# A graph layer on one core: 44 node columns a step instead of 40, three register loads on VectorE instead of two, and a gather ring of twenty

## The chip, the cores and the metric

The kernel runs on one core of a Trainium2 chip. The metric is device time in microseconds (us), from one launch to its end; the median of three runs of the kernel before is 1898.23 us (1897.33 to 1900.16). The profile was taken from one further execution. The engines are TensorE (PE, its weight loads PEld), VectorE (DVE), ScalarE (ACT), GpSimd (POOL) and SyncE (SP). Each engine has a sequencer, which reads the instruction stream in order, executes register loads, register arithmetic and semaphore instructions itself, and passes the rest to its engine; the profile marks the sequencer's own entries with a q (DVEq).

## The reference

One message-passing layer over 12500 nodes of 64 features and 212500 edges that are sorted by destination (`dst`), a residual and a layer norm:

```python
msg_in = concatenate([nodes[row], nodes[col], edge_features])        # 64 + 64 + 32 per edge
messages = relu(msg_in @ mW1 + mb1) @ mW2 + mb2                      # 160 -> 128 -> 64
aggregated = segment_sum(messages, col, num_segments=12500)
upd_in = concatenate([nodes, aggregated])
y = relu(upd_in @ uW1 + ub1) @ uW2 + ub2
out = layernorm(x + y)                                               # row = src, col = dst
```

Everything is float32. `mW2` is applied after the sum over edges, so the kernel sums the 128 hidden values of each edge and counts the edges of each node.

## The kernel before

**Tiling.** The 212500 edges are cut into G = 554 groups of 384 edges (TG = 3 tiles of 128). Because the edges are sorted by destination, the destinations of a group lie in a window of W = 32 nodes. Four groups (SB = 4) make a block, whose transposed edge features are loaded by one DMA into a buffer `own.st` (a ring of BLOCKS = 3).

**Two ways for source features to arrive.** The 64 features of each edge's source node come by an indirect DMA from GpSimd, one for each tile of 128 edges (`gather`, L149), into the ring `own.s`, from where TensorE turns (transposes) them (L341) and ScalarE copies them into `own.st` (L351). For some groups, listed in `COPIED`, the first tile is not gathered. Its 128 columns of 64 features are copied one at a time, 64 partitions by 4 bytes, from the node table `own.xc`, which holds all node features transposed in SBUF, straight to their place in `own.st` (`fetch`: VectorE at L503, ScalarE at L505). Where a column is to be read from is known only at run time, so a register load (L490) first brings a number of addresses from SBUF into the engine's registers, one register for one column. A step k from BEGIN = 18 on copies COLS = 40 columns: VectorE 8 and 12 (`VCOLS`, two register loads), ScalarE 12 and 8 (`ACOLS`). A copied group so comes every 128/40 = 3.2 steps, until step 544 (G - SHORT); `COPIED` has 164 groups, and 3 x 553 + 2 - 164 = 1497 gathers are left. The addresses of SPAN = 8 steps come together by a small DMA on SyncE's queue (`indexes`) and are made into byte addresses by one VectorE instruction (`addresses`, L473).

**A step.** In the main loop step k gives TensorE one run of instructions: the turn of group k, the hidden layer of group k - 2 (L366, then Relu on ScalarE, L377) and the sums of group k - 4 (L394, and the counts of edges L399). Only the last instruction of a run is waited for. On VectorE a step is, in program order:

- in one step of four, `places`: a register load of four window positions (L301) and four copies of window columns (L308);
- a piece of the update of a finished chunk of 512 nodes, if one is due (`update`, L413 to L458; 25 chunks in all);
- `add` of group k - 4: the sums are added into `agg` (L406), the counts into a row of `own.xc` (L407), both at a position held in a register;
- in one step of four, the copies of four window matrices (L320);
- the one-hot of group k + 2 (L329), which TensorE needs in step k + 2;
- `fetch(k)`: a load of 8 registers and 8 copies, a load of 12 registers and 12 copies. ScalarE's 12 and 8 are emitted right behind.

**Rings and waits.** `gather(k + AHEAD)` is emitted at the end of step k, with AHEAD = 4 and RING = AHEAD + 4 = 8 buffers; it waits for the turn of an earlier group that used the buffer, taken at the second of a pair of groups (L157). Waits between engines are partly set by hand (`after`) and otherwise found by the framework, which also orders the two engines' writes into the same `own.st` buffer. The last SHORT = 10 steps copy no columns and run the sums and hidden parts closer together.

Of the kernel before, what the change touches and what calls it, by code (L numbers as in the profile page):

```python
# [14 lines left out]
AF = mybir.ActivationFunctionType  # L15
ALU = mybir.AluOpType
# [7 lines left out]
D = 64  # L24
# [7 lines left out]
GE = TG * P  # L32
G = (E + GE - 1) // GE
SB = 4
AHEAD = 4
RING = AHEAD + 4
BLOCKS = 3
NW = 2 * SB
# [8 lines left out]
TIMES = 4  # L47
BEGIN = 18
CHECKED = 8
VCOLS = (8, 12)  # L50
ACOLS = (12, 8)
COLS = sum(VCOLS + ACOLS)
SPAN = 8
# [55 lines left out]
def ordered(ctx: ExitStack, tc: tile.TileContext, a, own, ok):  # L109
# [25 lines left out]
    def after(first, *others):  # L135

        tc.declare_no_dep(first.ins, group="quiet", reason="waits for the last of a step")
        for i in others:
            tc.add_manual_dep(
                first.ins, i.ins.name,  # L140
                mybir.DependencyInfo(mybir.DependencyClass.Sync, mybir.DependencyReason.DATA),
                reason="the kernel's own rings",
            )
        return first

    def gather(g):
        s = own.s[g % RING]
        loads[g] = [
            nc.gpsimd.indirect_dma_start(  # L149
                out=s[:p, j, :D], out_offset=None, in_=x[:, :],  # L150
                in_offset=bass.IndirectOffsetOnAxis(
                    ap=src_sb[:p, g * TG + j : g * TG + j + 1], axis=0),
            )
            for j, p in enumerate(tiles_of(g)) if j or g not in columned
        ]
        for i in loads[g]:
            after(i, *([turn_by[g // 2 * 2 + 1 - RING]] if g >= RING else []))  # L157


    iota_i = const.tile([P, W], F32, name="iota_i")  # L160
# [174 lines left out]
    def turn(g, ps):  # L335


        s = own.s[g % RING]
        xt = ps[0][: D + W, :GE]
        did = [  # L340
            nc.tensor.transpose(xt[:, j * P : j * P + p], s[:p, j, :], ident[:p, :p])  # L341
            for j, p in enumerate(tiles_of(g))
        ]

        def copy(step):
            t, c, n = columns(g)
            turn_by[g] = step
            whole = [(slice(D + W), slice(n))]
            apart = [(slice(D, D + W), slice(P)), (slice(D + W), slice(P, n))]
            copies = [  # L350
                after(nc.scalar.activation(t[r, c : c + n][:, m], xt[r, m], AF.Copy), step)  # L351
                for r, m in (apart if g in columned else whole)
            ]
            if g >= BLOCKS * SB:
                after(copies[0], hidden_by[g - BLOCKS * SB])
            copy_by[g] = copies
            return copies

        return did, [*loads.pop(g), places_by[g]], copy
# [27 lines left out]
    def sums(g, ps):  # L387
        h, s = own.h[g % NH], own.s[g % RING]
        sizes = tiles_of(g)
        sg = ps[2][:, : TIMES * W].rearrange("p (t w) -> p t w", w=W)  # L390
        counted = ps[2][0:1, TIMES * W :][:, :W]
        did = []
        for j, p in enumerate(sizes):
            did.append(nc.tensor.matmul(  # L394
                sg, h[:p, j, :],
                s[:p, j, D:].unsqueeze(1).to_broadcast([p, TIMES, W]),
                start=j == 0, stop=j == len(sizes) - 1))
        for j, p in enumerate(sizes):
            did.append(nc.tensor.matmul(counted, own.one[:p], s[:p, j, D:],  # L399
                                        start=j == 0, stop=j == len(sizes) - 1))  # L400

        def add(step):
            sums_by[g] = step
            at = bass.ds(starts.pop(g), W)
            return [
                after(nc.vector.tensor_tensor(agg[:, at], sg[:, 0, :], agg[:, at], ALU.add), step),  # L406
                after(nc.vector.tensor_tensor(xc[D : D + 1, at], counted,  # L407
                                              xc[D : D + 1, at], ALU.add), step),
            ]

        return did, [*relu_by[g], *copy_by[g]], add

# [49 lines left out]
    def indexes(i):  # L462

        n = min(SPAN * COLS, P * len(COPIED) - i * SPAN * COLS)
        if n > 0:
            indices[i] = ixp.tile([1, SPAN * COLS], I32, name="index")
            nc.sync.dma_start(indices[i][:, :n], a["src_copied"][:, i * SPAN * COLS :][:, :n])

    def addresses(i):

        if i in indices:
            t = indices[i][:, : min(SPAN * COLS, P * len(COPIED) - i * SPAN * COLS)]
            nc.vector.tensor_scalar(t, t, 4.0, float(own.at), ALU.mult, ALU.add)  # L473

    def fetch(k):

        i, n = divmod(k - BEGIN, SPAN)
        if i < 0:
            return
        if n == 0:  # L480
            indexes(i + 1)
        if n == SPAN - 2:
            addresses(i + 1)
        c0 = (k - BEGIN) * COLS
        for engine, count in [*((ET.DVE, c) for c in VCOLS), *((ET.Activation, c) for c in ACOLS)]:
            count = min(count, P * len(COPIED) - c0)
            if count <= 0:
                return
            b = c0 - i * SPAN * COLS
            _, v = nc.values_load_multi_w_load_instructions(  # L490
                indices[i][0:1, b : b + count], engines=[engine],
                min_val=own.at, max_val=own.at + 4 * (N - 1),
                skip_runtime_bounds_check_because="a source is one of the nodes",
            )
            for q, at in zip(range(c0, c0 + count), v):
                g, c = COPIED[q // P], q % P
                t, first_c, _ = columns(g)
                o = t.bitcast(U8)[:D, 4 * (first_c + c) : 4 * (first_c + c + 1)]
                x_at = xc_bytes[:D, bass.ds(at - own.at, 4)]
                by = columns_by.setdefault(g, {})  # L500
                new = engine not in by
                if engine == ET.DVE:
                    by[engine] = nc.vector.tensor_copy(o, x_at)  # L503
                else:
                    by[engine] = nc.scalar.activation(o, x_at, AF.Copy)  # L505
                after(by[engine], *([hidden_by[g - BLOCKS * SB]] if new else []))
            c0 += count

    waiting = [(closes, update(base, p, n)) for base, p, n, closes in PLAN]
    now = []  # L510
# [13 lines left out]
    def step(*work):  # L524


        parts, used = [], []
        for part, g in work:
            ps, old = own.ps[g % 2], users[part][g % 2]
            parts.append((part, g, *part(g, ps)))  # L530
            used += old
        did = [i for p in parts for i in p[2]]
        after(did[0], *used, *(i for p in parts for i in p[3]))
        copies = None
        for part, g, *_ in parts:
            if part is sums:
                for b in [b for b in xws if (b - 1) * SB <= g][:1]:
                    last, copies = windows(b, own.ps[g % 2][2][:, (TIMES + 1) * W :][:, :H])
                    did.append(last)
        for i in did[:-1]:  # L540
            tc.no_tile_sem_insts.add(i.ins.name)
            tc.add_to_no_dep_group("quiet", i.ins)
        for part, g, _, _, follow in parts:
            if part is sums:
                step_update(g)
            users[part][g % 2] = follow(did[-1])
            if part is sums and copies:
                copies()
                users[part][g % 2] += [wm_by[b * SB + i] for i in range(min(SB, G - b * SB))]
# [6 lines left out]
    windows(0, ups.tile([H, CH], F32, name="u_ps")[:, :H], False)[1]()  # L556
    indexes(0)
    made = summed = 0

    for k in range(G):  # L560
        if k < BITS:
            bit(k)
        if k == CHECKED:
            addresses(0)
            combined()
            ordered_edges()
            early.close()
            up = ctx.enter_context(tc.tile_pool(name="upd", bufs=2))
        if k % SB == 2:
            inputs(k // SB + 2)  # L570
        if k % SB == 1:
            places(k // SB + 1)
        if k < G - SHORT:
            step((turn, k), *([(hidden, k - 2)] if k > 1 else []),
                 *([(sums, k - 4)] if k > 3 else []))
            made, summed = max(0, k - 1), max(0, k - 3)
        else:

            step((turn, k))
            for _ in range(2):  # L580
                if summed < made:
                    step((sums, summed))
                    summed += 1
            for _ in range(2):
                if made <= k:
                    step((hidden, made))
                    made += 1
        onehot(k + 2)
        fetch(k)
        if k + AHEAD < G:  # L590
            gather(k + AHEAD)
    while summed < G:
# [332 lines left out]
```

## Time and profile before

| what | us |
|---|---|
| median of three runs | 1898.23 |
| the profiled execution, its own time | 1895.48 |
| its span, first to last instruction | 1893.5 |
| VectorE busy | 1492.9 (79%) |
| ScalarE busy | 1550.7 (82%) |
| GpSimd busy | 1417.6 (75%) |
| TensorE busy | 1361.4 (72%) |

The granted TensorE clock is 0.969 on average. The rows of the profile name an instruction by its line, its engine, what it writes and reads, and its count; "idle before" is the time in which the engine stood still ahead of these instructions, with what ended it ("issue": nothing that the profile shows). The sequencer's instructions do not count as busy.

### The profile page before, as it was taken

To read this page: it belongs to the slowest core of one execution; us is meant where nothing else is said; L and a number is where in the kernel's file an instruction comes from. 1 tells how busy PE (TensorE), PEld (TensorE's weight loads), DVE (VectorE), ACT (ScalarE), POOL (GpSimd) and SP (SyncE) were. 2 spreads that over 40 slices of the span, in tenths; PEclk is the share of its full clock that TensorE was granted. 3 is DMA by queue.
4 is the path that set the end of the run, shared out by engine and by line. 5 is a ranking of instruction groups with operands and counts; after the bars stand their busy time and mean duration, and the time that the engine had idled before them with its cause. 6 is when DMAs were issued, how large, how long until landed. Compare 5 with 4: busy or idle time off the path is not lost. (4 is left out here: it accounts for less than half of the span.)

```text
span 1893.5 us, 58044 instructions
## 1 busy us (share of the span) xinstructions
PE 1361.4 (72%) x12209; PEld 1193.4 (63%) x12209; DVE 1492.9 (79%) x13761; ACT 1550.7 (82%) x11818; POOL 1417.6 (75%) x1504
## 2 busy tenths in 40 slices
PE   3776777677777777677676776877767767767777
PEld 3666666666666666666665666666666656666665
DVE  3578888778888788887888878878888887888873
ACT  3489889888888888988988888889888888898882
POOL 7777777777777777777777777777777777777774
PEclk9999999999999999999999999999999999999999
DMA  6322222222222222222222222222222222222221
GB/s 136 73 46 45 46 48 44 50 43 48 46 45 48 47 43 50 45 46 44 48 50 43 48 46 45 46 48 44 50 44 47 47 48 44 47 44 50 44 47 29
DMA packets 68440, 92.50 MB, mean 49 GB/s; under 512 B 30893, under 2 KB 38350, under 8 KB 68078
## 3 DMA queue, kind: packets, MB, share of 16 engines
q0 software_dynamic: 47904, 49.12, 14.7%
q1 hardware_dynamic: 19260, 39.12, 7.4%
q14 instruction: 260, 2.13, 0.4%
q8 instruction: 102, 1.67, 0.4%
q10 hardware_dynamic: 914, 0.46, 0.1%
HBM read 85.29 MB, written 3.20 MB: 47 GB/s over the span
## 5 line engine op out<-in xcount | busy, mean ns | idle before, releaser
L149 POOL DMA_INDIRECT own_s<-in_x,src_sb x1497 | 1416.8, 946 | 457.3 <-issue 407.5
L503 DVE COPY own_st<-own_xc 64x4 uint8 x10500 | 897.7, 190 | 231.0 <-issue 217.9
L505 ACT ACTIVATE own_st<-own_xc 64x4 uint8 x10492 | 1057.1, 194 | 18.2 <-issue 15.2
L341 PE MATMUL own_ps<-own_ident,own_s 128*96 128x128 f32 x1661 | 289.5, 285 | 496.0 <-DMA own_s<-in_x,src_sb 157.9
L341 PEld LDWEIGHTS own_ps<-own_ident,own_s 128*96 128x96 f32 x1661 | 169.3, 132 | 566.1 <-ACT own_h L377 240.7
L394 PE MATMUL own_ps<-own_s,own_h 128*128 128x128 f32 x3322 | 480.5, 283 | 4.1 <-ACT own_h L377 2.9
L366 PE MATMUL own_ps<-own_wm,own_st 128*128 128x128 f32 x3322 | 479.4, 283 | 0.0
L351 ACT ACTIVATE own_st<-own_ps 96x384 f32<-96x384 f32 (+2 forms) x718 | 293.2, 408 | 205.8 <-PE own_ps L399 104.7
L394 PEld LDWEIGHTS own_ps<-own_s,own_h 128*128 128x128 f32 x3322 | 432.6, 199 | 6.3 <-ACT own_h L377 4.7
L366 PEld LDWEIGHTS own_ps<-own_wm,own_st 128*128 128x128 f32 x3322 | 432.1, 199 | 1.4 <-issue 0.5
L377 ACT ACTIVATE own_h<-own_ps 128x384 f32<-128x384 f32 x553 | 263.9, 477 | 16.0 <-PE own_ps L366 16.0
L399 PE MATMUL own_ps<-own_s,own_one 128*1 128x32 f32 x3322 | 190.1, 194 | 0.0
L320 DVE COPY own_wm<-own_ps 32x128 f32<-32x128 f32 x550 | 156.9, 285 | 5.6
L399 PEld LDWEIGHTS own_ps<-own_s,own_one 128*1 128x1 f32 x3322 | 114.5, 84 | 69.4 <-issue 6.2
L329 DVE TENSOR_TENSOR own_s<-iota,dlc 128x96 f32<-128x96 f32 x554 | 142.4, 258 | 14.3 <-issue 0.2
L406 DVE TENSOR_TENSOR agg<-own_ps,agg 128x32 f32 x554 | 105.1, 190 | 59.5 <-PE own_ps L399 25.9
L407 DVE TENSOR_TENSOR own_xc<-own_ps,own_xc 1x32 f32 x554 | 101.2, 183 | 30.6 <-PE u_ps L425 11.4
L308 DVE COPY xw<-own_xc 66x32 f32 x554 | 73.0, 207 | 15.5 <-DMA own_xc<-in_xT 9.8
L315 PE MATMUL own_ps<-w1b,xw 66*128 66x128 f32 (+1 forms) x276 | 69.1, 333 | 0.0
L446 ACT ACTIVATE rstd<-mv,eps 128x4 f32<-128x4 f32 (+1 forms) x25 | 7.4, 297 | 55.3 <-DVE mv L444 55.3
L437 PE MATMUL u_ps<-u,u 128*128 128x64 f32 (+1 forms) x196 | 50.1, 399 | 0.5 <-ACT u L427 0.5
L437 PEld LDWEIGHTS u_ps<-u,u 128*128 128x128 f32 (+1 forms) x196 | 47.1, 324 | 2.2 <-ACT u L427 0.9
(62 smaller groups left out, 276.7 us busy)
## 6 DMA issues: line engine op xcount, KB each, us to landing
own_st<-in_efT SPq DMA_DIRECT2D x138, 192.0 KB
own_s<-in_x,src_sb POOLq DMA_INDIRECT x1497
xin<-in_x SPq DMA_DIRECT2D x24, 128.0 KB
out<-o SPq DMA_DIRECT2D x24, 128.0 KB
own_xc<-in_xT SPq DMA_DIRECT2D x12, 179.2 KB
index<-in_src_copied SPq DMA_DIRECT2D x65, 1.2 KB
dlc_i<-in_dst_cols SPq DMA_DIRECT2D x1, 831.0 KB
own_xc<-in_xT SPq DMA_DIRECT2D x4, 179.5 KB
```

The source lines that it names most:

```text
L149: nc.gpsimd.indirect_dma_start(out=s[:p, j, :D], out_offset=None, in_=x[:, :], in_offset=bass.IndirectOffsetOnAxis(ap=src_sb[:p, g * TG + ...
L320: c = nc.vector.tensor_copy(wm[g % NW][D : D + W, :], wp[i * W : (i + 1) * W, :])
L329: places_by[g] = nc.vector.tensor_tensor(own.s[g % RING][:, :, D:], iota.unsqueeze(1).to_broadcast([P, TG, W]), dlc[:, g * TG : (g + 1) * ...
L341: nc.tensor.transpose(xt[:, j * P : j * P + p], s[:p, j, :], ident[:p, :p])
L351: after(nc.scalar.activation(t[r, c : c + n][:, m], xt[r, m], AF.Copy), step)
L366: nc.tensor.matmul(pre[:p, j, :], t[:, c + j * P : c + j * P + p], wm[g % NW], start=True, stop=True)
L377: relu_by[g] = [nc.scalar.activation(h, pre, AF.Relu)]
L394: did.append(nc.tensor.matmul(sg, h[:p, j, :], s[:p, j, D:].unsqueeze(1).to_broadcast([p, TIMES, W]), start=j == 0, stop=j == len(sizes) - 1))
L399: did.append(nc.tensor.matmul(counted, own.one[:p], s[:p, j, D:], start=j == 0, stop=j == len(sizes) - 1))
L406: after(nc.vector.tensor_tensor(agg[:, at], sg[:, 0, :], agg[:, at], ALU.add), step),
L503: by[engine] = nc.vector.tensor_copy(o, x_at)
L505: by[engine] = nc.scalar.activation(o, x_at, AF.Copy)
```

## The change

`COLS` goes from 40 to 44: VectorE copies 8, 8 and 8 columns a step in place of 8 and 12, ScalarE 12 and 8 as before. The three VectorE parts no longer stand together at the end of the step: the first is emitted between the two additions of `add`, the second after the step's window copies and ahead of the one-hot, the third after the one-hot. `indexes` and `addresses` of the next eight steps move behind the step's columns. AHEAD becomes 16 and the ring 20 buffers, and a gather waits for the turn of exactly the group that last used its buffer. The copies into `own.st` (L351, L503, L505) are put into a group within which the framework makes no dependencies, apart from the one on the same engine's preceding copy; the waits set by hand for TensorE's read of the buffer stay.

```diff
-AHEAD = 4
+AHEAD = 16
 RING = AHEAD + 4
-VCOLS = (8, 12)
+VCOLS = (8, 8, 8)
 ACOLS = (12, 8)
...
+    before = {}
+
+    def ordered_by_steps(i):
+
+        engine = i.ins.engine
+        tc.declare_no_dep(i.ins, group="features", keep=before.get(engine, []),
+                          reason="TensorE's step has read what the last turn of the ring wrote")
+        tc.add_to_no_dep_group("features", i.ins)
+        before[engine] = [i.ins]
+        return i
...
-            after(i, *([turn_by[g // 2 * 2 + 1 - RING]] if g >= RING else []))
+            after(i, *([turn_by[g - RING]] if g >= RING else []))
...
-                after(nc.scalar.activation(t[r, c : c + n][:, m], xt[r, m], AF.Copy), step)
+                ordered_by_steps(
+                    after(nc.scalar.activation(t[r, c : c + n][:, m], xt[r, m], AF.Copy), step))
...
-            return [
-                after(nc.vector.tensor_tensor(agg[:, at], sg[:, 0, :], agg[:, at], ALU.add), step),
-                after(nc.vector.tensor_tensor(xc[D : D + 1, at], counted,
-                                              xc[D : D + 1, at], ALU.add), step),
-            ]
+            a = after(nc.vector.tensor_tensor(agg[:, at], sg[:, 0, :], agg[:, at], ALU.add), step)
+            if between:
+                between.pop()()
+            return [a, after(nc.vector.tensor_tensor(xc[D : D + 1, at], counted,
+                                                     xc[D : D + 1, at], ALU.add), step)]
...
-    def fetch(k):
+    def fetch(k, *parts):
...
-        if n == 0:
-            indexes(i + 1)
-        if n == SPAN - 2:
-            addresses(i + 1)
-        c0 = (k - BEGIN) * COLS
-        for engine, count in [*((ET.DVE, c) for c in VCOLS), *((ET.Activation, c) for c in ACOLS)]:
+        all_parts = [*((ET.DVE, c) for c in VCOLS), *((ET.Activation, c) for c in ACOLS)]
+        for part in parts:
+            engine, count = all_parts[part]
+            c0 = (k - BEGIN) * COLS + sum(c for _, c in all_parts[:part])
...
-                after(by[engine], *([hidden_by[g - BLOCKS * SB]] if new else []))
-            c0 += count
+                ordered_by_steps(after(by[engine],
+                                       *([hidden_by[g - BLOCKS * SB]] if new else [])))
...
         if k < G - SHORT:
+            between.append(lambda: fetch(k, 0))
             step((turn, k), *([(hidden, k - 2)] if k > 1 else []),
                  *([(sums, k - 4)] if k > 3 else []))
             made, summed = max(0, k - 1), max(0, k - 3)
+            if between:
+                between.pop()()
+            fetch(k, 1)
...
         onehot(k + 2)
-        fetch(k)
+        if k < G - SHORT:
+            fetch(k, *range(2, len(VCOLS + ACOLS)))
+            if k >= BEGIN and (k - BEGIN) % SPAN == 0:
+                indexes((k - BEGIN) // SPAN + 1)
+            if k >= BEGIN and (k - BEGIN) % SPAN == SPAN - 2:
+                addresses((k - BEGIN) // SPAN + 1)
         if k + AHEAD < G:
             gather(k + AHEAD)
```

More of the change, by code (lines that the diff above doesn't have):

```diff
@@ L558, in ordered @@
     made = summed = 0
+    between = []
     for k in range(G):
```

## The prediction

> **What bounds the kernel now.** I read the page first, then the gathers by their line, the stretches of the run, and VectorE's groups within the stretch that copies columns.
>
> ```profile
> PE 1361.4 (72%) x12209; PEld 1193.4 (63%) x12209; DVE 1492.9 (79%) x13761; ACT 1550.7 (82%) x11818; POOL 1417.6 (75%) x1504
> DVE  3578888778888788887888878878888887888873
> POOL 7777777777777777777777777777777777777774
> ...
> L505 ACT ACTIVATE own_st<-own_xc 64x4 uint8 x10492 | 1057.1, 194 | 18.2 <-issue 15.2
> ```
>
> No engine is over 82% busy, but GpSimd's digits are level throughout, which is how an engine looks that never stops.
>
> ```profile
> L149 POOL DMA_INDIRECT own_s<-in_x,src_sb x1497: 901/944/1612, 2.9 to 1874.8; - x188
> ...
> POOL own_s L149 <- issue: 407.5, 1337, 0.3
> ```
>
> The 1497 gathers start between 2.9 and 1874.8 us: 1871.9/1496 = 1.2513 us from one to the next, and the pause between two is never over 0.3 us. GpSimd is full. At 40 columns a step it asks for (3 - 40/128) x 1.2513 = 3.363 us a step.
>
> ```profile
> core 0: us, PE busy (x) PEld busy (x) DVE busy (x) ACT busy (x) POOL busy (x), PEclk, DMA share, GB/s
> 80.50:1846.50 1766.00, 1284.51 (x11580) 1128.05 (x11580) 1443.02 (x13533) 1513.13 (x11756) 1335.65 (x1413) 0.97 0.22 46
> 0.00:80.50 80.50, 43.06 (x357) 38.35 (x358) 33.90 (x151) 26.77 (x37) 59.77 (x68) 0.96 0.53 116
> 1846.50:1893.50 47.00, 33.84 (x273) 27.05 (x272) 15.96 (x79) 10.78 (x26) 22.22 (x24) 0.92 0.14 29
> ```
>
> The stretch that copies columns lasts 1766.0 us. VectorE made 10500 copies, 20 a step, so it holds 525 steps of 3.364 us, which is the gathers' rate. Now VectorE's groups within that stretch:
>
> ```profile
> L503 DVE COPY own_st<-own_xc 64x4 uint8 x10500 | 897.7, 190 | 231.0 <-issue 217.9 <-ACT own_h L377 3.0 <-ACT own_st L351 0.5
> L320 DVE COPY own_wm<-own_ps 32x128 f32<-32x128 f32 x524 | 149.5, 285 | 5.3
> L329 DVE TENSOR_TENSOR own_s<-iota,dlc 128x96 f32<-128x96 f32 x525 | 135.3, 258 | 13.7 <-issue 0.2
> L406 DVE TENSOR_TENSOR agg<-own_ps,agg 128x32 f32 x525 | 99.5, 190 | 18.5 <-PE u_ps L424 9.7 <-PE own_ps L315 6.2 <-PE own_ps L399 1.8
> L407 DVE TENSOR_TENSOR own_xc<-own_ps,own_xc 1x32 f32 x525 | 95.9, 183 | 29.1 <-PE u_ps L425 10.7 <-DVE agg L406 1.0 <-issue 0.7
> L439 DVE TENSOR_TENSOR y<-u_ps,xin 128x256 f32<-128x256 f32 x23 | 9.8, 424 | 18.3 <-PE u_ps L437 18.2
> ```
>
> If the gathers alone set the pace, VectorE would stand at L406, its first wait for TensorE's step. It stands there 18.5 us in 525 steps. Its idle time is 1766.0 - 1443.0 = 323 us, of which 217.9 lie ahead of the columns and wait for nothing. So VectorE is nearly full too: at most (1766.0 - 18.5)/525 = 3.33 us a step are its own. **The two engines are in balance**, and relief for GpSimd that is paid by VectorE must be costed on VectorE.
>
> **What VectorE does in the unnamed time.** The chain of waits between 1831 and 1847 us runs on VectorE alone:
>
> ```profile
> 1832.39 0.21 DVE own_st L503 x3
> 1832.61 0.49 issue
> 1833.10 0.51 DVE own_st L503 x6
> ...
> 1839.89 0.07 DVEq L301
> ...
> 1840.80 0.20 DVE agg L406
> ```
>
> Beside it stand the register loads L490 that began in three narrow windows of this stretch, the load of four registers, and the eight copies in the order of time:
>
> ```profile
> L490 DVEq TENSOR_LOAD <-index x1: 598/598/598, 1831.3 to 1831.3; - x1
> L490 DVEq TENSOR_LOAD <-index x1: 844/844/844, 1832.2 to 1832.2; - x1
> L490 DVEq TENSOR_LOAD <-index x1: 595/595/595, 1833.9 to 1833.9; - x1
> ...
> L301 DVEq TENSOR_LOAD <-start_i x139: 340/344/594, 13.8 to 1863.6; - x139
> ...
> 1831.94 0.67 DVE L503 COPY own_st<-own_xc 64x4 uint8 x8
> ```
>
> A load of 8 takes 0.595 us, of 12 0.844, of 4 0.344: some 0.062 us a register and 0.095 for the load. Between the first two loads (1831.3 + 0.598 to 1832.2, starts to a tenth) the sequencer passed on 8 copies in 0.3 us, 0.04 each. VectorE executes one in about 0.07 (eight in 0.67, the last being 0.15 long). Then the 12-load keeps the sequencer to 1833.04, the queued copies run out at 1832.61, and VectorE idles 0.49 us until 1833.10. **The load is serial time of the sequencer**, hidden only as far as queued work lasts.
>
> **The sequencer's sum for a step.** From 1833.04 to the next load at 1833.9 are 0.87 us for 12 copies (0.48), both additions with their register arithmetic and the one-hot: 0.39 for the latter. `places` takes from 1839.89 to 1840.80, 0.91 us in one step of four, 0.23 a step; four window copies at 0.04 in one step of four, 0.04. Before: 0.595 + 0.844 + 20 x 0.04 + 0.39 + 0.23 + 0.04 = 2.90 us. After: 3 x 0.595 + 24 x 0.04 + 0.39 + 0.23 + 0.04 = **3.41 us**. Splitting the 12-load and adding four registers costs 3 x 0.595 - 1.439 = 0.35; four copies more, 0.16.
>
> The gathers would then need (3 - 44/128) x 1.2513 = 3.324 us a step. The bare sequencer sum is already over that, and over today's 3.364.
>
> **What comes on top.** Before, VectorE's own 3.33 less 2.90 leaves 0.43 us a step that my terms do not name: updates, a full queue behind slow instructions such as the window copies (285 ns each), and short pauses. Carried whole this gives 3.84. The engine's side says about the same: 1443.0/525 = 2.75 us busy plus four copies at 897.7/10500 = 0.0855 is 3.09; the unnamed idle was 217.9/525 = 0.415 for a 12-load, so the queue covers 0.43 of a load, an 8-load behind eight copies leaves about 0.165, and three leave 0.50; with 0.20 of other idle (323 - 217.9 over 525) that is 3.79. But where the sequencer is late more often the queue is full less often, so part of the 0.43 goes. What surely stays are the updates' 15 instructions a chunk at 0.04 (23 chunks over 525 steps, 0.03) and a pause of the stream. One such stands in the chain between two copies that no load parts:
>
> ```profile
> 1834.73 0.22 issue
> 1834.95 0.30 DVE own_st L503 x3
> ```
>
> I estimate these at 0.1 a step, so the low end is 3.41 + 0.03 + 0.1 = 3.54. I take the middle of 3.54 and 3.79, **3.66 us a step**, since both ends are derived from the same rows and neither side's waiting vanishes.
>
> The Trainium skill, "DMA: Bandwidth & Descriptors", Latency and other measured facts, gives a register load a floor of about 600 ns. The 344 ns of L301 disagrees and the measurement decides; if each load cost 0.6 whatever its size, a third would add 0.6 in place of 0.35, and 524 x 0.25 = 131 us would come on top.
>
> **The other parts.** Columns: 44 a step until step 544 allow 180 copied groups (180 x 128/44 = 523.6, so 524 steps), 16 gathers fewer, worth 20 us if GpSimd still decided. I set it at nothing, because VectorE is the later one; if it isn't, the 20 us come back (rival 1). The ring of twenty only lets GpSimd run further ahead; with the gathers early, it covers nothing that is waited for. Its 16 opening groups issue 48 gathers, of which the first four groups' were issued at once before; GpSimd is busy from 2.9 us in either order, so nothing moves. The dropped waits:
>
> ```profile
> ACT own_st L505 <- DVE own_s L329: 2.3, 4, 0.6
> ...
> PE own_ps L341 <- DVE own_st L503: 27.4, 22, 2.3
> ...
> index<-in_src_copied SPq DMA_DIRECT2D x65, 1.2 KB
> ```
>
> Between the column engines all visible waits are 3.0 + 0.5 us on VectorE and 2.3 on ScalarE: under 6 us, and not on VectorE's sequencer. I take nothing; both ends are 0 and -6. TensorE's 27.4 us of waiting for VectorE's columns will grow, and it is the same lateness, not a second price. The index DMA and L473 move within a step; eight steps lie between the DMA and its use, and the additions' order matters to TensorE only two steps later (same bank). Moving the counts' addition behind eight copies can cost the engine up to one copy's 0.15 us, inside the 3.54 to 3.79.
>
> **Sum.** Column stretch 524 x 3.66 = 1917.8 us; one step becomes an uncopied one of about 2.9 (the sequencer's sum without columns is shorter, the earlier rate with 40 is longer; the choice is worth 1 us). Opening 80.5 and end 47.0 stay. Against the profiled execution's 1895.48: 1895.5 + 1917.8 + 2.9 - 1766.0 = 2050.2. The median of the runs lies 2.75 us above that execution, so 2053.
>
> **Rivals.**
>
> 1. *GpSimd still decides.* A load would have to run beside the dispatch of instructions around it, leaving VectorE with 24 copies at 0.07 and its other work, under 3.324 us. Then 524 x 3.324 + 2.9 - 1766.0 = -21: 1877 with the offset. For it: VectorE is 79% busy, and 3.09 us busy a step would fit. Against it: the 0.49 us gap that ends just when the 12-load ends. It decides from a VectorE step of 3.324 us downwards. The Trainium skill, "Advanced Engine Details and Errata", Sequencer Loop, says other instructions can be read and queued while a control instruction executes; the trace shows no copy of a load starting before its load's end, so this gets little.
> 2. *The bare sequencer sum.* The queue of VectorE never fills and nothing pauses: 524 x 3.41 + 2.9 - 1766.0 = +24, 1922 with the offset. For it: three small loads are spaced evenly. Against it: the 0.43 us that exist today.
> 3. *Everything adds.* Each new load finds a short queue, the counts' addition waits for the copies ahead of it, and nothing of the 0.43 goes: 524 x 3.84 + 2.9 - 1766.0 = +249, 2147. For it: VectorE's balance today. Against it: the first 8-load is fully hidden now, so spreading covers something.
> 4. *No effect:* VectorE at 3.36 a step, which no sum here gives.
>
> **How the numbers follow.** Forecast 0.62 (1982 to 2120), rival 1 0.07, rival 2 0.12, rival 3 0.17, rival 4 0.02. Low reaches rival 2's neighbourhood, 1930, and high most of rival 3, 2130; about 0.15 is left out. Faster than by 0.2% (about what a measurement here tells from no change) is rival 1 alone: 0.07; within it 0.02; slower 0.91.
>
> **What would show it.** In the new profile: 1572 VectorE loads L490, all near 0.595 us; over 0.3 us of idle "issue" time a step ahead of L503; gather pauses far over 0.3 us that TensorE's turn ends; almost no wait at L406; columns over some 1900 us. Each step of the sum falls if the loads are shorter, if other instructions start while a load runs, or if the gathers still follow every 1.25 us: then VectorE's step was under 3.324 and I am wrong.

## The result, and the profile after

The changed kernel takes 2136.42 us (median of 4 runs, 2133.23 to 2139.39), before 1897.78 in the same measurement: a ratio of 1.126, 95% interval 1.1245 to 1.1274. It is 239 us slower; 155 were forecast. The direction and the engine were right, the size was not: the time lies 6 us above 2130, the high end of the range. Ten of the runs reported below were made on four chips on which the kernel before itself took 2580 to 2677 us, and no price is drawn from them.

The stretches of the run after the change, cut at the first and the last column as before (columns: length, then each engine's busy time and count, clock, DMA):

```profile
0.00:79.56 79.56, 43.78 (x357) 38.88 (x357) 33.73 (x150) 27.23 (x38) 59.20 (x68) 0.96 0.49 117
79.56:2083.75 2004.19, 1401.87 (x11549) 1229.59 (x11550) 1623.29 (x15606) 1519.94 (x11740) 1345.35 (x1421) 0.90 0.17 41
2083.75:2135.50 51.75, 38.76 (x306) 31.45 (x304) 16.69 (x83) 11.89 (x29) 0.00 (x0) 0.86 0.04 11
```

The profiled span grew by 2135.5 - 1893.5 = 242.0 us: 238.2 in the stretch that copies columns (2004.2 for 1766.0), 4.8 in the end, -0.9 in the opening. The last columns are copied one step earlier, so the end holds one step more (306 matmuls in place of 273); that is the uncopied step for which the prediction added 2.9 us. So the miss lies in the column stretch, for which 1917.8 us were forecast. Its 524 steps make **3.825 us a step**, for 3.364 before and 3.66 forecast. VectorE's groups in this stretch of the changed kernel, and its register loads:

```profile
L513 DVE COPY own_st<-own_xc 64x4 uint8 x12576 | 1120.8, 186 | 336.0 <-issue 281.3 <-DVE agg L417 2.4
L331 DVE COPY own_wm<-own_ps 32x128 f32<-32x128 f32 x524 | 149.6, 285 | 5.3
L340 DVE TENSOR_TENSOR own_s<-iota,dlc 128x96 f32<-128x96 f32 x524 | 130.9, 250 | 1.8
L417 DVE TENSOR_TENSOR agg<-own_ps,agg 128x32 f32 x524 | 103.0, 197 | 4.3 <-PE own_ps L326 1.5 <-PE u_ps L436 1.5 <-issue 0.3
...
L500 DVEq TENSOR_LOAD <-index x1572: 591/595/849, 78.9 to 2082.4; - x197
```

The wait for TensorE at the first addition (L417 is the old L406) fell from 18.5 to 4.3 us: VectorE sets the pace. There are 1572 loads of 0.595 us, as expected. Idle time ahead of the columns is 336.0/524 = 0.64 us a step, before 231.0/525 = 0.44. VectorE's busy time grew more than its idle time: from 1443.0 to 1623.3 us, 3.10 a step, as four copies at 0.0855 had it. GpSimd, which before never paused for over 0.3 us but for one opening wait, now stands for the ring (waits of the changed kernel, then its gathers):

```profile
POOL own_s L160 <- PE own_ps L411: 201.5, 160, 5.0
POOL own_s L160 <- PE own_ps L326: 50.6, 52, 4.8
...
L160 POOL DMA_INDIRECT own_s<-in_x,src_sb x1481: 902/947/1640, 2.9 to 2051.1; - x186
```

The 16 gathers are saved, and the last one starts 176 us later than before (1874.8). VectorE in the order of time, changed kernel, two steps:

```profile
1017.55 0.17 DVE L417 TENSOR_TENSOR agg<-own_ps,agg 128x32 f32 x1
1018.09 0.66 DVE L513 COPY own_st<-own_xc 64x4 uint8 x8 [0.37 <-issue]
1018.78 0.18 DVE L420 TENSOR_TENSOR own_xc<-own_ps,own_xc 1x32 f32 x1
1019.18 0.68 DVE L513 COPY own_st<-own_xc 64x4 uint8 x8 [0.22 <-issue]
1019.78 0.24 DVE L340 TENSOR_TENSOR own_s<-iota,dlc 128x96 f32<-128x96 f32 x1
1020.14 0.66 DVE L513 COPY own_st<-own_xc 64x4 uint8 x8
1020.71 0.17 DVE L417 TENSOR_TENSOR agg<-own_ps,agg 128x32 f32 x1
1021.28 0.66 DVE L513 COPY own_st<-own_xc 64x4 uint8 x8 [0.39 <-issue]
```

Ahead of each of the first two parts of eight VectorE stands and waits for nothing but its own load: these loads begin at 1017.4 and 1018.5 us and take 0.59 and 0.60. The third part has a gap of 0.1 us, too short to be printed. The first load, behind the single addition, leaves the longest gap. That holds for the whole stretch: the idle time ahead of the first parts is 202.5 us (0.39 a step), ahead of the second 76.2, ahead of the third 51.2.

### The profile page after: what moved, and what is told of

Same layout as the page of the kernel before. It is cut to its first block, busy times and chain, and to the rows that moved or that the text cites. A ratio compares the mean times of both kernels' runs of the same rounds, so it can differ in the third digit from the quotient of the medians.

```text
span 2135.5 us, 60828 instructions
## 1 busy us (share of the span) xinstructions
PE 1484.4 (70%) x12209; PEld 1299.9 (61%) x12209; DVE 1673.7 (78%) x15837; ACT 1559.1 (73%) x11806; POOL 1404.5 (66%) x1488
## 5 line engine op out<-in xcount | busy, mean ns | idle before, releaser
L513 DVE COPY own_st<-own_xc 64x4 uint8 x12576 | 1120.8, 186 | 336.0 <-issue 281.3
L352 PE MATMUL own_ps<-own_ident,own_s 128*96 128x128 f32 x1661 | 311.4, 301 | 615.9 <-ACT own_h L389 277.9
L352 PEld LDWEIGHTS own_ps<-own_ident,own_s 128*96 128x96 f32 x1661 | 178.2, 139 | 692.2 <-ACT own_h L389 311.3
L406 PE MATMUL own_ps<-own_s,own_h 128*128 128x128 f32 x3322 | 534.8, 304 | 4.1 <-ACT own_h L389 3.6
L378 PE MATMUL own_ps<-own_wm,own_st 128*128 128x128 f32 x3322 | 517.9, 298 | 0.0
L406 PEld LDWEIGHTS own_ps<-own_s,own_h 128*128 128x128 f32 x3322 | 485.8, 220 | 6.2 <-ACT own_h L389 5.2
L378 PEld LDWEIGHTS own_ps<-own_wm,own_st 128*128 128x128 f32 x3322 | 469.0, 213 | 2.1 <-issue 0.5
L411 PE MATMUL own_ps<-own_s,own_one 128*1 128x32 f32 x3322 | 199.6, 200 | 0.0
L411 PEld LDWEIGHTS own_ps<-own_s,own_one 128*1 128x1 f32 x3322 | 120.9, 86 | 78.0 <-issue 24.1
L417 DVE TENSOR_TENSOR agg<-own_ps,agg 128x32 f32 x554 | 108.8, 196 | 48.3 <-PE own_ps L411 22.0
```

Of the source, the lines that this page charges most:

```text
L378: nc.tensor.matmul(pre[:p, j, :], t[:, c + j * P : c + j * P + p], wm[g % NW], start=True, stop=True)
L406: did.append(nc.tensor.matmul(sg, h[:p, j, :], s[:p, j, D:].unsqueeze(1).to_broadcast([p, TIMES, W]), start=j == 0, stop=j == len(sizes) - 1))
L417: a = after(nc.vector.tensor_tensor(agg[:, at], sg[:, 0, :], agg[:, at], ALU.add), step)
```

## The experiments

The theory to be tested: VectorE's step is its sequencer's time, above all register loads, plus the time in which the sequencer is held by slow instructions. The rivals: the ring or the dropped waits cost the time; a load has a fixed price; the 24 executed copies are too long; the new places cost it. Each time below is a single run, to be compared with 2136.4 us, whose four runs lie within some 3 us of it. The kernel before, run beside each, took 1895.8 to 1898.8 us; the changed kernel was not run beside them.

**Ring and dropped waits alone.** Columns as before the change:

```diff
-VCOLS = (8, 8, 8)
+VCOLS = (8, 12)
...
-            between.append(lambda: fetch(k, 0))
...
-            if between:
-                between.pop()()
-            fetch(k, 1)
...
-            fetch(k, *range(2, len(VCOLS + ACOLS)))
+            fetch(k, *range(len(VCOLS + ACOLS)))
```

> The changed kernel with VectorE's columns as before (8 and 12, both at the end of the step): ring of twenty, exact ring wait and dropped waits alone, once more. VectorE theory: 1885 to 1905 us. If the ring, the order of gathers or the missing waits cost the time, above 1950 us.

Measured: 1898.28 us, the kernel before beside it 1896.67. Its gathers:

```profile
L160 POOL DMA_INDIRECT own_s<-in_x,src_sb x1497: 898/944/2112, 3.0 to 1877.1; - x188
```

GpSimd is full again, from 3.0 to 1877.1 us. The ring of twenty, the exact ring wait and the dropped waits together cost nothing and bring nothing here; all 239 us lie in VectorE's columns and their places.

**Without the third load.** The third part's copies read fixed columns of the node table, so the features of these edges are not those of their sources; the 24 copies are executed all the same.

```diff
+            if part == 2:
+                v = [own.at + 4 * (c0 + j) % 4096 for j in range(count)]
+            else:
                 _, v = nc.values_load_multi_w_load_instructions(
```

> The changed kernel without the third register load (the last 8 VectorE columns of a step are read from fixed places of the node table), beside a run of the kernel before near 1898 us: in the first try the kernel before itself took 2677 us. Sequencer theory: 0.595 us a step goes, 3.23 is under the gathers' 3.324, so 1875 to 1900 us. If the loads are hidden and VectorE's 24 executed copies are what is too long, the time stays above 2080 us.

Measured: 1920.76 us. The columns of this kernel, and the wait for the ring:

```profile
L516 DVE COPY own_st<-own_xc 64x4 uint8 (+1 forms) x12576 | 1107.6, 187 | 173.7 <-issue 155.8 <-DVE agg L417 0.5
...
L160 POOL DMA_INDIRECT own_s<-in_x,src_sb x1481 | 1400.9, 946 | 452.5 <-issue 341.1 <-DMA own_s<-in_x,src_sb 87.2 <-PE own_ps L411 16.5
```

One load less takes 215.7 us off, 0.41 a step, with the same number of copies: the rival of the executed copies falls. But the gathers did not take over at 1877: TensorE's steps hold GpSimd for only some 20 us, and VectorE's step, 3.825 - 0.41 = 3.41 us, is still longer than the gathers' 3.324. Of the load's 0.595 us, 0.18 do not come back. The idle time ahead of the columns fell by 162 us, three quarters of the gain.

**Four columns less, still three loads in the new places** (`VCOLS = (8, 8, 4)`, 40 columns in all).

> The changed kernel with 8, 8 and 4 columns on VectorE (three loads, 40 columns in all), once more beside a kernel before near 1898 us. By the sequencer's sum 3.825 - 0.41 = 3.41 us a step, 1922 us; if only 0.7 of it reaches the step, 3.54 and 1990 us. If the number of loads or their new places is what costs, over 2050 us.

Measured: 1967.38 us, between the two sizes. The loads and the columns:

```profile
L500 DVEq TENSOR_LOAD <-index x1575: 339/593/842, 79.5 to 1916.6; - x197
...
L513 DVE COPY own_st<-own_xc 64x4 uint8 x10500 | 953.8, 186 | 328.3 <-issue 287.5 <-DVE agg L417 24.3
```

Four columns, a load shorter by 0.25 us and four copies less, are worth 169.0/524 = 0.32 us a step. What is left over the first experiment is 1967.4 - 1898.3 = 69 us: the same 20 columns in three places and three loads in place of two at the end. So the four columns are 169 of the 239 us, and splitting and spreading the loads about 70. For VectorE alone they cost at least that, since in the first experiment the gathers set the pace and VectorE's own step may be shorter.

**Two loads of 12 in place of three of 8** (`VCOLS = (12, 12)`, 44 columns).

> The changed kernel with 12 and 12 columns on VectorE, 44 in all, in two loads, once more. By the registers a load takes: 0.095 us a step less, 50 us, 2087 us; 2102 if 0.7 of it reaches the step. If a load has a fixed price whatever its size, the 0.415 us of the run without the third load come back and the time is near 1920 us. If longer loads leave longer gaps than short ones hide, no gain or a loss: 2135 or more.

Measured: 2124.34 us, 12 us less than three loads. No case of the expectation hit: a fixed price of a load falls (it would have brought over 200 us), but of the 0.095 us that the loads are shorter only 0.02 arrive. The idle row shows where a part of the rest went:

```profile
L500 DVEq TENSOR_LOAD <-index x1048: 842/848/1087, 79.2 to 2069.9; - x175
...
L513 DVE COPY own_st<-own_xc 64x4 uint8 x12576 | 1052.4, 187 | 357.5 <-issue 344.8 <-DVE agg L417 4.5
```

The idle time ahead of the columns is 357.5 us, some 20 more than with three short loads: a longer load outlasts the queue by more.

**The three parts at the end of the step.** The edit of `fetch`'s places from the first experiment, with 8, 8 and 8.

> The changed kernel with all three VectorE parts of 8 at the end of the step in place of three places, a third time. If the places are worth nothing to a sequencer that is the later one: 2136 us, within 15. If they hide part of the loads behind the additions and the one-hot: 2150 to 2190. If they are what costs (the counts' addition behind eight copies), under 2110.

Measured: 2092.87 us, so **the new places cost 44 us**. VectorE in the order of time with all parts at the end, one step:

```profile
1019.44 0.19 DVE L417 TENSOR_TENSOR agg<-own_ps,agg 128x32 f32 x1
1019.67 0.18 DVE L420 TENSOR_TENSOR own_xc<-own_ps,own_xc 1x32 f32 x1
1019.88 0.26 DVE L340 TENSOR_TENSOR own_s<-iota,dlc 128x96 f32<-128x96 f32 x1
1020.35 0.71 DVE L513 COPY own_st<-own_xc 64x4 uint8 x8 [0.21 <-issue]
1021.27 0.66 DVE L513 COPY own_st<-own_xc 64x4 uint8 x8 [0.20 <-issue]
1022.17 0.88 DVE L513 COPY own_st<-own_xc 64x4 uint8 x8 [0.25 <-issue]
...
L513 DVE COPY own_st<-own_xc 64x4 uint8 x12576 | 1109.2, 188 | 239.2 <-issue 211.9 <-DVE own_s L340 0.5
```

Here the first load stands behind three slow instructions, for which the sequencer needs 0.39 us by the prediction's reading and VectorE 0.63, and so more of it is hidden. In the changed kernel it stands behind copies and one addition of 0.17 us. The idle time ahead of the columns is 239.2 us in place of 336.0, of which 44 us reach the time. By parts it is 52.7, 81.1 and 99.1 us, in the changed kernel 202.5, 76.2 and 51.2: the first load gains 150 us by the old place, the other two lose 53. Why a load behind eight copies and an addition leaves more idle time than one behind eight copies alone (202.5 us, here 81.1) was not separated; the addition's register arithmetic, which the sequencer executes, stands ahead of that load too.

**Without the copies of the window matrices** after the first two blocks; the hidden layer then uses old windows.

```diff
+                if g >= NW:
+                    wm_by[g] = wm_by[g - NW]
+                    continue
                 c = nc.vector.tensor_copy(wm[g % NW][D : D + W, :], wp[i * W : (i + 1) * W, :])
```

> The changed kernel without the copies of the window matrices (L331) after the first two blocks, four in one step of four, 0.295 us each on the engine. If VectorE's engine is what such a step waits for, while its sequencer stands before a full queue, about 0.7 us in four steps go, 0.17 a step, 90 us: 2045 us; in full, 1.18 in four steps, 1980 us. If only their passing on counts (0.04 us a step, the prediction's term), 21 us: 2116.

Measured: 2040.94 us, 95.5 less, 0.18 a step. One copy a step was 0.04 in the prediction's sum. The columns of this kernel:

```profile
L516 DVE COPY own_st<-own_xc 64x4 uint8 x12576 | 1127.3, 188 | 374.5 <-issue 303.7 <-DVE agg L420 2.9
```

The idle time ahead of the columns rose by 38.5 us, from 336.0: the window copies had hidden some of the loads, so of their 149.6 us of VectorE's time only about two thirds come back.

**Without the updates' layer norm.** The output is what stands ahead of it; 13 VectorE instructions a chunk go.

```diff
-            for k in range(n):
-                nc.vector.bn_stats(stats[:p, k], y[:p, k])
-                nc.vector.bn_aggr(mv[:p, k], stats[:p, k])
...
-            nc.vector.reciprocal(rstd[:p, :n], rstd[:p, :n])
...
-                nc.vector.tensor_scalar(
-                    o[:p, k], y[:p, k], mv[:p, k, 0:1], rstd[:p, k : k + 1],
```

> The changed kernel without the updates' layer norm: 13 VectorE instructions a chunk less (two for each of four statistics, the reciprocal, four scalings), some 3.0 us of VectorE time a chunk, so the output is what stands ahead of the layer norm. If an update's engine time adds in full while the sequencer stands before a full queue: 23 x 3.0 = 69 us less, 2068 us. If only their passing on counts, as the prediction's low end had it (0.04 each): 23 x 0.52 = 12 us less, 2125.

Measured: 2077.15 us, 59.3 less, so most of the 69 us of VectorE's own time and five times what passing the instructions on would cost. VectorE's busy time fell by 55.9 us (1673.7 to 1617.8), and the idle time ahead of the columns stayed:

```profile
L501 DVE COPY own_st<-own_xc 64x4 uint8 x12576 | 1124.2, 186 | 337.7 <-issue 279.3 <-DVE agg L417 4.2
```

**Ten runs where the kernel before takes 2580 to 2677 us.**

| kernel | us there | the kernel before beside it |
|---|---|---|
| ring and dropped waits alone | 2454.6, 2458.9 | 2677.2, 2658.7 |
| third part from fixed places | 2504.8 | 2677.2 |
| 8, 8, 4 columns | 2500.3 | 2658.7 |
| 8, 6, 6 columns | 2678.7 | 2677.2 |
| 12, 12 columns | 2572.1, 2584.7, 2558.7 | 2677.2, 2658.7, 2639.0 |
| three parts at the end | 2501.0, 2455.1 | 2639.0, 2580.3 |

The ring and the dropped waits alone, at 2454.6 us, are 0.918 of the kernel before there (interval 0.910 to 0.927), where at 1898 us they bring nothing. All kernels of the table have them, and all but 8, 6, 6 are faster than the kernel before beside them. What makes that difference was not separated, and nothing is concluded from it. The expectations of these runs, in the order of the table, were written for a chip on which the kernel before takes 1898 us, and none can be judged here:

> The changed kernel with VectorE's columns as before (8 and 12, both at the end of the step): ring of twenty, exact ring wait and dropped waits alone. If VectorE's sequencer set the changed kernel's pace (a load 0.095 + 0.062 us a register, 0.04 us a copy passed on), it is back at about 3.33 us a step, the gathers decide again at 3.363, and the time is that of before: 1890 to 1905 us. If the ring, the order of gathers or the missing waits cost the time, it stays above 1950 us.

> The changed kernel with VectorE's columns as before (8 and 12, both at the end of the step): ring of twenty, exact ring wait and dropped waits alone, again, beside a kernel before near 1898 us. If VectorE's sequencer made the change slow, the time is that of before, 1890 to 1905 us; a gain of up to 1% where the longer ring keeps the gathers ahead of VectorE's uneven steps is the most it can bring, as the gathers still take 1497 x 1.25 us. If the ring, the order of gathers or the missing waits cost the time, it stays above 1950 us.

> The changed kernel without the third register load: the last 8 VectorE columns of a step are read from fixed places of the node table, the 24 copies stay. Sequencer theory: 0.595 us a step goes, 3.23 is under the gathers' 3.324, so 1875 to 1900 us. If the loads are hidden and VectorE's 24 executed copies are what is too long, the time stays above 2080 us.

> The changed kernel with 8, 8 and 4 columns on VectorE: three loads in the new places, 20 columns, 40 in all. By the sequencer's sum a load of 4 takes 0.344 in place of 0.595 and four copies less are 0.16: 3.825 - 0.41 = 3.41 us a step, 1922 us; if as in the run without the third load only 0.7 of it reaches the step (0.415 of 0.595), 3.54 and 1990 us. If the number of loads or their new places is what costs, over 2050 us.

> The changed kernel with 8, 6 and 6 columns on VectorE: three loads in the new places, but 20 columns, 40 in all. Sequencer theory: loads 0.595 + 2 x 0.47 = 1.53 in place of 1.785, copies 0.80 in place of 0.96, so 3.825 - 0.41 = 3.41 us a step and 1922 us (1905 to 1945). If the third load as such costs its whole length, or the new places do, only the four copies' part comes back and the time stays above 2030 us.

> The changed kernel with 12 and 12 columns on VectorE: 44 in all, in two loads. Sequencer theory: 2 x 0.845 in place of 3 x 0.595 saves 0.095 us a step, 50 us, so 2087 us (2065 to 2115). If each load has a fixed price of about 0.6 us whatever its size, 0.6 us a step goes, the gathers decide and the time falls to 1880 us.

> The changed kernel with 12 and 12 columns on VectorE, 44 in all, in two loads, again. By the registers a load takes (0.062 each and 0.095): 0.095 us a step less, 2087 us, or 2102 if 0.7 of it reaches the step. If a load has a fixed price whatever its size, the 0.415 of the run without the third load come back and the time is near 1920 us.

> The changed kernel with 12 and 12 columns on VectorE, 44 in all, in two loads, on a chip where the kernel before takes near 1898 us. By the registers a load takes: 0.095 us a step less, 50 us, 2087 us; 2102 if 0.7 of it reaches the step. If a load has a fixed price whatever its size, the 0.415 us of the run without the third load come back and the time is near 1920 us. If longer loads leave longer gaps than short ones hide, no gain or a loss: 2135 or more.

> The changed kernel with all three VectorE parts of 8 at the end of the step, as before the change, in place of three places. If the places are worth nothing to a sequencer that is the later one: 2136 us, within 15. If they hide part of the loads behind the additions and the one-hot: 2150 to 2190. If they are what costs (the counts' addition behind eight copies), under 2110.

> The changed kernel with all three VectorE parts of 8 at the end of the step in place of three places, once more. If the places are worth nothing to a sequencer that is the later one: 2136 us, within 15. If they hide part of the loads behind the additions and the one-hot: 2150 to 2190. If they are what costs (the counts' addition behind eight copies), under 2110.

## Why the prediction was right in direction and wrong in size

*That GpSimd and VectorE are in balance, and VectorE pays:* right. With the old columns the gathers set the pace (1898.3), with four more on VectorE they wait 252 us for the ring.

*The prices of loads:* right in length, 0.595 us each, and too high as terms of the step: the sum counts a load in full, but removing one is worth 0.41 us, and four columns with a quarter of a microsecond of load are worth 0.32 where the sum has 0.41. *That the ring, the dropped waits and the 16 gathers are worth nothing here:* right. The kernel with the ring and the dropped waits alone takes 1898.28 us, and with the 16 gathers saved GpSimd only waits longer.

*The bare sum, 3.41 us a step:* held as a floor. The step measures 3.825, so 0.415 us were not in it.

*The step that failed* is the size of what comes on top of the bare sum: "where the sequencer is late more often the queue is full less often, so part of the 0.43 goes", and from it "the middle of 3.54 and 3.79". That left 0.25 us a step; the runs show 0.415. About half of what is missing is the part that was to go. With all parts at the end the step is 3.742 us, 0.33 over the bare sum, so of the 0.43 (itself an upper bound) only 0.10 went. The other half, 0.08, is the new places. The same seen from VectorE's side: busy 3.10 us a step (forecast 3.09), idle ahead of the columns 0.64 (forecast 0.50, with 0.165 for each load, where the first load leaves 0.39), other idle 0.09 (forecast 0.20). Its 3.79 was the better estimate, and taking the middle with 3.54 spoiled it. What single changes show of the 0.415:

| what | us a step | from |
|---|---|---|
| window copies beyond the 0.04 in the sum | 0.14 | 95.5/524 - 0.04 |
| layer norm of the updates | 0.11 | 59.3/524 |
| the new places of the loads | 0.08 | 43.5/524 |
| not separated: the updates' other two instructions, pauses of the stream and what else there is | 0.08 | 0.415 less the above |

Each was taken out alone and no run takes out two, so that they add up is not shown. Of the last line, the gaps between copies that no load parts are only 6 us in the stretch, 0.01 a step. The first two are slow instructions of VectorE. The account that fits is that while they run the sequencer gets ahead until it has to stand, and that afterwards it brings loads, the queue runs empty, and VectorE stands; how full the queue is, no row shows. What is shown is that the times overlap only in part: removing the layer norm brings back all of its busy time (59.3 us for 55.9), removing the window copies two thirds, removing a load 0.41 of 0.595 us. The prediction put the updates at 0.03 a step for passing on and the window copies at 0.04; taking them out is worth 0.11 (for 13 of 15 instructions) and 0.18.

The third was given no price of its own but was to lie "inside the 3.54 to 3.79", and rival 3 was held down by "spreading covers something". Here spreading uncovers: it puts the first load behind one addition. Without it (2092.9) the time would have been inside the range, and 3.742 us a step inside the bounds. As made, the kernel landed 11 us from rival 3, "everything adds", at 2147, which had 0.17; its condition, that nothing of the 0.43 goes, held in sum but not in its parts.

*Rival 1* fell with GpSimd's waits. *The counts' addition behind eight copies* starts 0.03 us after the last copy ends; that price is small, and the gap ahead of the copies is the cost of the place. *TensorE's waiting for VectorE's columns*, 27.4 us before, was to grow and fell to 1.5; it stood in no term of the sum.

## What to carry to other kernels

Where a sequencer's serial time (register loads, with 0.06 us a register here) and its engine's slow instructions both fill a step, do not take the larger of the two or a middle without a reason: here a sequencer's sum of 3.41 us and 3.10 us of busy engine made 3.74 to 3.83 us. A single removal brought back some 65 to 100% of the time of what was removed. A load is hidden by slow instructions passed on just ahead of it, so here the loads stood better together behind the slow ones, by 44 us; eight quick copies ahead of an 8-load left some 0.2 us of it open in the step shown. Where two engines are in balance, cost a shift of work on the one that receives it first: here 16 gathers, some 20 us, were bought for some 170 us of columns.

## What the runs showed of the hardware that was not expected

A load of registers depends on more than their number. In the kernel with 8, 6 and 6 columns, one run on one chip, the two loads of 6 take 0.82 and 1.41 us, more than its load of 8 with 0.594. Loads of that kernel in narrow windows:

```profile
L500 DVEq TENSOR_LOAD <-index x1: 819/819/819, 1000.4 to 1000.4; - x1
...
L500 DVEq TENSOR_LOAD <-index x1: 1414/1414/1414, 1001.5 to 1001.5; - x1
L500 DVEq TENSOR_LOAD <-index x1: 594/594/594, 1003.4 to 1003.4; - x1
```

Counted from 0, they begin at the 8th and the 14th of a step's 40 addresses; all other loads here start at and take multiples of four. The chip is not the cause: in the kernel with loads of 8 and 12 on the same chip, 524 of the 1050 take 0.6 us and 483 take 0.8. What of the two decides, the start or the number, was not tried.

The pauses between copies that no load parts are regular. In the changed kernel there are 27 of over 0.1 us, and each stands a multiple of 128 instructions behind the one before it, counted over VectorE and its sequencer. What happens there no row names.

The granted TensorE clock fell from 0.969 to 0.901 although TensorE was busy for 70% of the span in place of 72%. It was 0.969 again with the old columns (1898.28 us). What lowers it was not tried.
